# A four-layer graph-attention kernel: the setup in an order of its own

## The chip, the core and the metric

The kernel runs on one core of one Trainium2 chip. The metric is the device time of one execution in microseconds, as a median over several runs. The kernel before takes 2730.86 us (median of 3 runs, 2729.93 to 2731.75). A profile of one execution shows a span of 2728.8 us.

The core has five engines [...]: TensorE (PE, matrix products and transposes; its weight loads are counted apart as PEld), VectorE (DVE), ScalarE (ACT), GpSimd (POOL) and SyncE (SP). SyncE issues most transfers here; ScalarE can issue them too. [...]

## What is computed

`x` is 16 graphs of 1024 nodes with 256 features, `adj` is one 1024 x 1024 matrix of int32, shared by all graphs. Four layers follow each other; each normalises x, applies a ReLU, runs a graph attention and adds the result to x. Layer 0 looks like this; the others differ in heads (4, 1, 4, 1), in the slope, in the test on `adj` and in the last function:

```python
h = jnp.maximum(_layernorm(x, axis=-1), 0.0)
q = (h @ W).reshape(B, N, H, D)
e_src = jnp.einsum('bnhd,d->bnh', q, a_src)
e_dst = jnp.einsum('bnhd,d->bnh', q, a_dst)
e = e_src[:, :, None, :] + e_dst[:, None, :, :]
e = jnp.where(e >= 0, e, ALPHA * e)
e = jnp.where(mask, e, NEG_INF)        # adj > 0 in layers 0, 1; adj != 0 in layers 2, 3
attn = jax.nn.softmax(e, axis=2)
h_prime = jnp.einsum('bijh,bjhd->bihd', attn, q)
x = x + jax.nn.elu(h_prime)            # relu in layer 3
```

## The kernel before

**Steps and streams.** One step is one layer of one graph, 64 steps in all. Four graphs are in work at a time ("streams"); `order_of_steps` interleaves them, so the order begins with layer 0 of streams 0, 1, 2, then layer 1 of stream 0, layer 0 of stream 3, layer 1 of stream 2, layer 2 of stream 0.

**A step** has three parts. Its *preparation* (L159) has 20 pieces: statistics of x on VectorE and ten small operations on GpSimd (`stats`, L166), normalising on ScalarE (`xn`, L193), transposes on TensorE with the ReLU on ScalarE (`hT`, L201, L202), the products with the weights (`project`, L213, evacuated by ScalarE into `whx` and `sd`), then exponentials of the attention logits (`factors`) and a small transpose whose result goes to DRAM (`grow`) and comes back as a row broadcast to all partitions (`gs`, L258; copied into PSUM as `g`, L264). Its *aggregation*: VectorE makes tiles of attention weights `w` (L269, 128 x 1024, eight to a head) out of `g`, the column factors and a mask; TensorE multiplies them with `whx` (L285). Its *finish* (L306 to L328) divides, applies the last function and adds to x.

**Order by hand.** All this is emitted under a manual schedule. Index 8n + k is the group k of step n, eight to each step. An agenda gives each piece of a preparation its index (`agenda_of`), normally one to two steps ahead; `emit_tiles` sends tiles of w ahead as far as 18 buffers (`WBUFS`) allow; `finish` of a step lies in the first groups of the next. The two first preparations have index -99, so both are emitted whole before the first group.

**The setup** stands ahead of this loop and is not part of the manual schedule. First, for each of the four layers: load the weights W, load the two attention vectors broadcast to all partitions (`a_bc`, on ScalarE's queue), make extra columns of W out of them on VectorE (four products, L104, and four sums, L106), and get a bound on the logits: a square (`sq`, L111), two products with a matrix of ones (`pn`, L114), a maximum, a root on GpSimd and three small products, which give `cbias`, `nbias`, `rbias`. Then the masks, in eight row blocks of `adj`: load 128 rows, clamp to -1, 0, 1 as `sgn` (L134), eight transposes into PSUM (L137), and two compares on VectorE (L139), greater than zero for layers 0 and 1 and not equal to zero for layers 2 and 3. Last, the loads of x for the four streams. The two setup parts have pools of their own, released before the pools of the main part are made, so that memory of the first is used again by the second.

Of the kernel before, what the change touches and what calls it, by code (L numbers as in the profile page):

```python
# [23 lines left out]
F32 = mybir.dt.float32  # L24
BF16 = mybir.dt.bfloat16
I32 = mybir.dt.int32
U8 = mybir.dt.uint8
AF = mybir.ActivationFunctionType
ALU = mybir.AluOpType
AX = mybir.AxisListType  # L30
PSUM = bass.MemoryType.PSUM

P = 128
EPS = 1e-5
SHIFT = 60.0
STREAMS = 4
WBUFS = 18
# [11 lines left out]
LAYERS = [  # L49
    (4, 0.2, 0, 0),  # L50
    (1, 0.2, 0, 0),
    (4, 0.2, 128, 1),
    (1, 0.01, 0, 1),
]
# [3 lines left out]
def kernel(ctx: ExitStack, tc: tile.TileContext, x, adj, ws, avs, out):  # L58
    nc = tc.nc
    B, N, F = x.shape  # L60
    C = N // P
    K = F // P
    HALF = C // 2

    const = ctx.enter_context(tc.tile_pool(name="const", bufs=1))

    ident = const.tile([P, P], F32, name="ident")
# [3 lines left out]
    half1 = const.tile([P, 1], F32, name="half1")  # L71
    nc.gpsimd.memset(half1, 0.5)
    ones = const.tile([P, P], F32, name="ones")
    nc.gpsimd.memset(ones, 1.0)

    masks = [const.tile([P, C, N], U8, name=f"mask{i}") for i in range(2)]
    wx = []
# [3 lines left out]
    nbias = [const.tile([P, 1], F32, name=f"nbias{l}") for l in range(len(LAYERS))]  # L81
    rbias = [const.tile([P, 1], F32, name=f"rbias{l}") for l in range(len(LAYERS))]
    cbias = [const.tile([P, 1], F32, name=f"cbias{l}") for l in range(len(LAYERS))]
    shift60 = const.tile([P, 1], F32, name="shift60")
    nc.gpsimd.memset(shift60, SHIFT)


    with tc.tile_pool(name="wprep", bufs=2) as wp, tc.tile_pool(
        name="wpsum", bufs=2, space=PSUM
    ) as wps:  # L90
        for l, (H, slope, hs, _) in enumerate(LAYERS):
            D = F // H
            nc.sync.dma_start(out=wx[l][:, :, 0:F], in_=ws[l].rearrange("(k p) f -> p k f", p=P))
            a_bc = wp.tile([P, 2, H, D], F32, name="a_bc")
            for part in range(2):
                nc.scalar.dma_start(
                    out=a_bc[:, part],
                    in_=bass.AP(tensor=avs[l].tensor, offset=avs[l].offset + part * D,
                                ap=[[0, P], [hs, H], [1, D]]),
                )  # L100
            for k in range(K):
                for part in range(2):
                    prod = wp.tile([P, H, D], F32, name="prod")
                    nc.vector.tensor_mul(  # L104
                        prod, wx[l][:, k, 0:F].rearrange("p (h d) -> p h d", h=H), a_bc[:, part])
                    nc.vector.tensor_reduce(  # L106
                        wx[l][:, k, F + part * H:F + (part + 1) * H], prod, AX.X, ALU.add)

            sq = wp.tile([P, K, H], F32, name="sq")
            wd = wx[l][:, :, F + H:F + 2 * H]  # L110
            nc.vector.tensor_tensor(sq, wd, wd, op=ALU.mult)  # L111
            pn = wps.tile([P, H], F32, name="pn")
            for k in range(K):
                nc.tensor.matmul(pn, lhsT=ones, rhs=sq[:, k, :], start=(k == 0),  # L114
                                 stop=(k == K - 1))
            bound = wp.tile([P, 1], F32, name="bound")
            nc.vector.tensor_reduce(bound, pn, AX.X, ALU.max)
            nc.gpsimd.tensor_tensor(bound, bound, half1, op=ALU.pow)
            nc.vector.tensor_scalar(cbias[l], bound, 16.01, None, op0=ALU.mult)
            nc.vector.tensor_scalar(nbias[l], bound, -16.01 * slope, None, op0=ALU.mult)  # L120
            nc.vector.tensor_scalar(rbias[l], bound, -16.01 * (1.0 - slope), SHIFT,
                                    op0=ALU.mult, op1=ALU.add)


    with tc.tile_pool(name="mprep", bufs=2) as mp, tc.tile_pool(
        name="mpsum", bufs=2, space=PSUM
    ) as mps:
        identb = mp.tile([P, P], BF16, name="identb", bufs=1)
        nc.vector.tensor_copy(identb, ident)
        for ic in range(C):  # L130
            a_raw = mp.tile([P, N], I32, name="a_raw")
            nc.sync.dma_start(out=a_raw, in_=adj[ic * P:(ic + 1) * P, :])
            sgn = mp.tile([P, N], BF16, name="sgn")
            nc.vector.tensor_scalar(sgn, a_raw, -1.0, 1.0, op0=ALU.max, op1=ALU.min)  # L134
            pm = mps.tile([P, C, P], BF16, name="pm")
            for jc in range(C):
                nc.tensor.transpose(pm[:, jc, :], sgn[:, jc * P:(jc + 1) * P], identb)  # L137
            for m, op in ((0, ALU.is_gt), (1, ALU.not_equal)):
                nc.vector.tensor_scalar(masks[m][:, :, ic * P:(ic + 1) * P], pm, 0.0, None, op0=op)  # L139

    xpool = ctx.enter_context(tc.tile_pool(name="xpool", bufs=STREAMS))
    prep = ctx.enter_context(tc.tile_pool(name="prep", bufs=2))
    small = ctx.enter_context(tc.tile_pool(name="small", bufs=4))
    work = ctx.enter_context(tc.tile_pool(name="work", bufs=2))
# [5 lines left out]
    L = len(LAYERS)  # L150
    steps = order_of_steps(B, L)
    xs = {}
    state = [dict() for _ in steps]

    def load(b):
        xs[b] = xpool.tile([P, C, F], F32, name="x")
        nc.sync.dma_start(out=xs[b], in_=x[b].rearrange("(c p) f -> p c f", p=P))
# [198 lines left out]
    def prepare(upto):  # L356

        while agenda and agenda[0][0] <= upto:
            _, n, piece, last = agenda.pop(0)
            piece()  # L360
            if last:
                done["prepared"] = n + 1

    def plan(n):
        new = preparation(n)
        agenda.extend((at, n, piece, i == len(new) - 1) for i, (at, piece) in enumerate(new))
        agenda.sort(key=lambda a: a[:2])
# [11 lines left out]
    def emit_tiles(upto, must=False):  # L379
        while done["tiles"] < min(upto, len(tiles)):  # L380
            i = done["tiles"]

            while done["g"] <= min(i + C // 2, len(tiles) - 1):
                n, h, _ = tiles[done["g"]]
                if n >= done["prepared"]:
                    if i < done["g"] or not must:
                        break
                    prepare(max(a[0] for a in agenda if a[1] == n))
                broadcast(n, h)
                done["g"] += C  # L390
                fetch_heads()
            if i >= done["g"]:
                return
            weights(*tiles[i])
            done["tiles"] += 1

    for b in range(STREAMS):
        load(b)
    last, agenda_of = {}, []
    for n, (b, l) in enumerate(steps):  # L400

        free = 8 * (last[b % STREAMS] + 1) + (8 if l == 0 else 5) if b % STREAMS in last else -99
        last[b % STREAMS] = n
        start = 8 * (n - 2)
        before = [LAYERS[steps[max(n - i, 0)][1]][0] for i in (0, 1, 2)]
        if before[2] == 1:
            kind = SOON if before[:2] == [4, 1] else AFTER_ONE
        else:
            kind = SOON if l == 0 else AFTER_FOUR
        if free > start + kind[0]:  # L410
            kind = LATE
            start = max(free, agenda_of[-1][0] + 5)
        agenda_of.append([start + k if n > 1 else -99 for k in kind])
        if n > 2:

            was = agenda_of[n - 1]
            assert agenda_of[n][2] >= was[4] and agenda_of[n][3] >= was[10]
    ending = []
    with tc.manual_schedule():
        for planned in (1, 2):  # L420
            plan(planned - 1)
            prepare(-1)
        for n in range(len(steps)):
            for k, (h, i0, per) in enumerate(groups(n)):
                while planned < len(steps) and agenda_of[planned][0] <= 8 * n + k:
                    plan(planned)
                    planned += 1
                emit_tiles(place[n, h, C - 1] + 1, must=True)
                aggregate(n, h, i0, per)
                if i0 + per == C:  # L430
                    done["free"] = place[n, h, C - 1] + 1
                while ending and ending[0][0] <= k:
                    ending.pop(0)[1]()
                prepare(8 * n + k)
                ahead = 6 if per > 1 else 3
                emit_tiles(min(done["tiles"] + ahead, done["free"] + WBUFS))
            for _, piece in ending:
                piece()
            ending = finish(n)
        for _, piece in ending:  # L440
            piece()
# [33 lines left out]
```

## Time and profile before

| what | value |
|---|---|
| median, lowest, highest of 3 runs | 2730.86, 2729.93, 2731.75 us |
| span of the profiled execution, mean clock of TensorE | 2728.8 us, 0.987 |
| TensorE busy | 2569.4 us (94%) |
| TensorE weight loads | 2269.7 us (83%) |
| VectorE busy | 1909.6 us (70%) |
| ScalarE busy | 1220.6 us (45%) |
| GpSimd busy | 985.5 us (36%) |
| largest group: products L285 | 1950.3 us, 36864 of them, 242 ns each |
| largest on VectorE: tiles w, L269 | 1544.6 us, 1280 of them, 1277 ns each |
| x of the four streams, issue | from 58.24 us, 4 of 1024 KB |

A busy share is an average over stages with different limits. Where it matters which engine sets the pace, one reads stretches of the time axis, and for each stretch the engine that has no idle time, or the wait that ends last.

### The profile page before, as it was taken

Reading aid. Unit: us, or ns where it says so; the run is one execution under the profiler, and the core shown is the slowest. Engines: PE = TensorE matmul, PEld = TensorE weight load, DVE = VectorE, ACT = ScalarE, POOL = GpSimd, SP = SyncE. Lnnn points to the kernel's source line nnn. Section 1 sums busy time; section 2 is a strip of 40 time slices with the busy share of each in tenths; the row PEclk is TensorE's granted clock in tenths of the full one; section 3 lists DMA queues with packets and bytes.
Section 4 is the critical chain, followed back from the end, with each engine's and each line's share of the span. In section 5 each row is a group of like instructions: output and inputs, shape, how many; then the busy total and the mean of one; then the engine's idle time right before and its main releaser. Section 6 shows DMA issues by size and latency. Waiting matters only on the chain.

```text
span 2728.8 us, 89586 instructions
## 1 busy us (share of the span) xinstructions
PE 2569.4 (94%) x40080; PEld 2269.7 (83%) x40080; DVE 1909.6 (70%) x2061; ACT 1220.6 (45%) x3329; POOL 985.5 (36%) x1230
## 2 busy tenths in 40 slices
PE   1699999999999999999999999999999999999998
PEld 1488888888888888888888888888888888788876
DVE  5396866667874878757877668747787567678752
ACT  0434445444454454454444544544435444444431
POOL 0224334334234344353242353433332443443321
PEclk9899999999999999999999999999999999999999
DMA  4110010011211111002211211002112110011111
GB/s 133 61 58 23 28 41 33 18 56 49 73 56 40 56 64 35 24 32 71 73 33 48 63 41 42 33 17 72 59 46 72 50 47 25 33 41 42 33 33 54
DMA packets 63679, 130.13 MB, mean 48 GB/s; under 512 B 6208, under 2 KB 41792, under 8 KB 63296
## 3 DMA queue, kind: packets, MB, share of 16 engines
q1 hardware_dynamic: 60608, 123.35, 13.6%
q8 instruction: 316, 5.18, 0.8%
q10 hardware_dynamic: 2688, 1.05, 0.1%
q14 instruction: 67, 0.55, 0.1%
HBM read 106.95 MB, written 17.43 MB: 46 GB/s over the span
## 4 chain that ended last, share of the span: by engine, by line
PE 81%; DVE 8%; ACT 4%; issue 4%; POOL 2%; DMA 1%; DVEq 0%; ACTq 0%; SPq 0%; POOLq 0%
PE acc L285 61%; PE pp L213 16%; DVE w L269 6%; PE pp L201 4%; ACT xn L193 1%; DVE bn L171 1%; POOL rstd L184 1%; DMA a_bc<-in_L_gnn_a 1%; ACT whx L215 1%; ACT e L319 0%; ACT g L264 0%; DVE mask L139 0%; ACT whx L219 0%; PE pp L240 0%; ACT whx L222 0%
## 5 line engine op out<-in xcount | busy, mean ns | idle before, releaser
L285 PE MATMUL acc<-whx,w 128*64 128x65 f32 x36864 | 1950.3, 242 | 42.2 <-DVE w L269 31.7
L285 PEld LDWEIGHTS acc<-whx,w 128*64 128x64 f32 x36864 | 1766.0, 145 | 225.4 <-issue 73.7
L269 DVE SCALAR_TENSOR_TENSOR w<-g,rcol,mask 128x1024 f32<-128x1024 f32 x1280 | 1544.6, 1277 | 482.8 <-ACT g L264 435.7
L289 ACT ACTIVATE y<-acc 128x260 f32<-128x260 f32 (+1 forms) x512 | 196.5, 384 | 1090.4 <-PE acc L285 1090.4
L213 PE MATMUL pp<-wx,hT 128*128 128x258 f32 (+1 forms) x2048 | 513.0, 394 | 5.6 <-ACT hT L202 4.4
L310 POOL TENSOR_TENSOR y<-y,r 128x1024 f32<-128x1024 f32 x128 | 242.3, 1897 | 614.2 <-DVE r L306 614.2
L213 PEld LDWEIGHTS pp<-wx,hT 128*128 128x128 f32 x2048 | 374.7, 191 | 76.4 <-ACT hT L202 7.3
L326 POOL TENSOR_TENSOR x<-x,e 128x1024 f32<-128x1024 f32 x96 | 226.7, 2366 | 278.0 <-DVE e L325 258.4
L224 POOL TENSOR_TENSOR whx<-whx 128x256 f32<-128x256 f32 x256 | 159.8, 629 | 457.0 <-ACT whx L222 456.1
L193 ACT ACTIVATE xn<-x,shift,rstd 128x256 f32<-128x256 f32 x512 | 264.0, 590 | 122.7 <-POOL shift L187 122.5
L325 DVE SCALAR_TENSOR_TENSOR e<-e,y 128x1024 f32<-128x1024 f32 x96 | 118.2, 1232 | 196.9 <-ACT e L319 196.9
L215 ACT ACTIVATE whx<-pp,nbias 128x4 f32<-128x4 f32 (+1 forms) x512 | 135.0, 264 | 165.3 <-PE pp L213 153.9
L201 PE MATMUL pp<-ident,xn 128*128 128x128 f32 x1024 | 158.3, 286 | 51.1 <-ACT xn L193 41.3
L201 PEld LDWEIGHTS pp<-ident,xn 128*128 128x128 f32 x1024 | 116.1, 143 | 91.2 <-ACT xn L193 52.0
L171 DVE BATCH_NORM_STATS2 bn<-x 128x6 f32<-128x256 f32 x512 | 173.2, 411 | 5.6 <-DMA x<-in_x 2.8
L264 ACT ACTIVATE g<-gs 128x1024 f32<-128x1024 f32 x160 | 162.3, 1018 | 5.2 <-DVE w L269 5.1
L202 ACT ACTIVATE hT<-pp 128x512 f32<-128x512 f32 x256 | 142.9, 592 | 16.1 <-PE pp L201 13.8
L178 POOL TENSOR_TENSOR dev<-bn 128x8 f32<-128x8 f32 x64 | 16.3, 255 | 308.4 <-DVE bn L171 308.4
L219 ACT ACTIVATE whx<-pp,whx 128x256 f32<-128x256 f32 x256 | 121.5, 474 | 0.0
L319 ACT ACTIVATE e<-e 128x1024 f32<-128x1024 f32 x96 | 100.8, 1050 | 30.1 <-POOL e L315 30.1
L184 POOL TENSOR_TENSOR rstd<-rstd,neghalf 128x8 f32<-128x8 f32 x64 | 106.6, 1666 | 5.0
L315 POOL TENSOR_SCALAR e<-y 128x1024 f32<-128x1024 f32 x96 | 99.9, 1040 | 8.5
(44 smaller groups left out, 552.7 us busy)
## 6 DMA issues: line engine op xcount, KB each, us to landing
gs<-grow SPq DMA_DIRECT2D x160, 512.0 KB
x<-in_x SPq DMA_DIRECT2D x16, 1024.0 KB
out<-x SPq DMA_DIRECT2D x32, 512.0 KB
a_raw<-in_adj SPq DMA_DIRECT2D x8, 512.0 KB
a_bc<-in_L_gnn_a ACTq DMA_DIRECT2D x8, 128.0 KB
wx<-in_L_gnn_W SPq DMA_DIRECT2D x4, 256.0 KB
grow<-gT SPq DMA_DIRECT2D x32, 16.0 KB
grow<-gT SPq DMA_DIRECT2D x32, 4.0 KB
```

Source lines behind the costliest of these rows:

```text
L171: nc.vector.bn_stats(bn[:, c, :], xs[b][:, c, :])
L193: nc.scalar.activation(xn[:, q, :], xs[b][:, c, :], AF.Identity, bias=st["shift"][:, c:c + 1], scale=st["rstd"][:, c:c + 1])
L201: nc.tensor.transpose(pt[:, q, :], st["xn", half][:, q, k * P:(k + 1) * P], ident)
L213: nc.tensor.matmul(pw, lhsT=st["hT", half][:, k, q * P:(q + 1) * P], rhs=wx[l][:, k, :], start=(k == 0), stop=(k == K - 1))
L215: nc.scalar.activation(whx[:, c, :, D], pw[:, F + H:F + 2 * H], AF.Exp, bias=nbias[l], scale=slope)
L224: nc.gpsimd.tensor_tensor(whx[:, c, :, 0:D], whx[:, c, :, 0:D], whx[:, c, :, D:D + 1].to_broadcast([P, H, D]), op=ALU.mult)
L264: nc.scalar.activation(g, state[n]["gs", h], AF.Copy)
L269: nc.vector.scalar_tensor_tensor(w, state[n]["g", h], state[n]["rcol"][:, jc, h:h + 1], masks[LAYERS[steps[n][1]][3]][:, jc, :], op0=ALU.m ...
L285: nc.tensor.matmul(acc[o % P:o % P + cols, q, :], lhsT=st["w", h, jc][:, o:o + cols], rhs=st["whx"][:, jc, h, :], start=(jc == 0), stop=(j ...
L289: nc.scalar.activation(st["y"][:, i0:i0 + per, h, :], acc, AF.Copy)
L310: nc.gpsimd.tensor_tensor(yh, yh, r[:, :, None].to_broadcast([P, HALF * H, D]), op=ALU.mult)
L326: nc.gpsimd.tensor_add(xh, xh, e)
```

## The change

The setup is taken apart and emitted under the manual schedule as well, in an order of its own. Five things change:

1. x of stream 0 is the first transfer; then come W and the vectors of layer 0 and x of stream 1. The streams 2 and 3 are loaded after step 1's preparation, together with the weights of the other layers.
2. `adj` is loaded in column blocks (128 columns of all rows, in rows of 512 bytes) on ScalarE's queue. A block goes straight into one row of the mask.
3. Only the first mask is made by a compare on VectorE. The second, not equal to zero, is the square of the same values (-1, 0, 1), made by ScalarE out of the same PSUM tile.
4. The mask blocks are interleaved with the preparation of step 0: three blocks before its first transposes, three between its parts, two after it. Step 1's preparation follows in halves, with the eight first tiles of w between them.
5. The extra columns and bounds of layers 1, 2 and 3 are made in the loop: vectors, columns and bound of layer 1 at index 1, 2, 3; of layer 2 at 29, 30, 31 (the last groups of step 3); of layer 3 at 45, 46, 47 (the last groups of step 5). Their small constants go to GpSimd.

The separate pools are gone: blocks of `adj` and `sgn` use buffers of `w`, the transposed block a PSUM buffer of `acc`, the vectors a buffer of `e`, the bound one of `pp`. The purpose is that the engines work side by side in the setup, and that what the first step doesn't need comes later.

```diff
-    with tc.tile_pool(name="wprep", bufs=2) as wp, tc.tile_pool(
...
-    with tc.tile_pool(name="mprep", bufs=2) as mp, tc.tile_pool(
...
-            for m, op in ((0, ALU.is_gt), (1, ALU.not_equal)):
-                nc.vector.tensor_scalar(masks[m][:, :, ic * P:(ic + 1) * P], pm, 0.0, None, op0=op)
+    def weight_columns(l):
...
+        def vectors():
+            st["a"] = prep.tile([P, HALF, H, D], F32, name="e")
+            for part in range(2):
+                nc.sync.dma_start(
...
+        def columns():
...
+        def bound():
+
+            pn = ps_p.tile([P, H], F32, name="pp")
...
+        def fetch_block():
+            st["raw"] = work.tile([P, C, P], I32, name="w", bufs=WBUFS)
+            nc.scalar.dma_start(out=st["raw"], in_=adj.rearrange("(c p) j -> p c j", p=P)[
+                :, :, jc * P:(jc + 1) * P])
...
+        def mask():
+            pm = st["pm"].rearrange("p c i -> p (c i)")
+            nc.vector.tensor_scalar(masks[0][:, jc, :], pm, 0.0, None, op0=ALU.is_gt)
+            nc.scalar.activation(masks[1][:, jc, :], pm, AF.Square)
...
-    for b in range(STREAMS):
-        load(b)
...
-        agenda_of.append([start + k if n > 1 else -99 for k in kind])
+        agenda_of.append([start + k for k in kind] if n > 1 else [-2] * 10 + [-1] * 10)
...
+        load(0)
+        load_weights(0)
+        layer[0][0]()
+        for jc in range(C):
+            blocks[jc][0]()
+        load(1)
+        nc.vector.tensor_copy(identb, ident)
+        first = [piece for _, piece in preparation(0)]
+        first[0]()
+        first[1]()
+        layer[0][1]()
+        layer[0][2]()
+        first[2]()
+        first[3]()
+        for jc in range(3):
+            for piece in blocks[jc][1:]:
+                piece()
+
+        for i, jc in ((4, 3), (6, 4), (10, 5), (12, None), (14, None)):
...
+        for piece in first[16:]:
+            piece()
+        for jc in range(6, C):
+            for piece in blocks[jc][1:]:
+                piece()
+        done["prepared"] = 1
+        plan(1)
+        planned = 2
+        prepare(-2)
+        emit_tiles(C, must=True)
+        prepare(-1)
+        for i in range(1, STREAMS):
+            load_weights(i)
+            if i > 1:
+                load(i)
+
+        for l, at in ((1, 1), (2, 8 * 3 + 5), (3, 8 * 5 + 5)):
+            for i, piece in enumerate(layer[l]):
+                later[at + i] = piece
...
+                if 8 * n + k in later:
+                    later[8 * n + k]()
                 prepare(8 * n + k)
```

## The prediction

> **What bounds the kernel now.** I read the page's slices first, to see where TensorE is not full; then a table of busy times by stretch over the first 300 us; then VectorE in order of time; then the waits of the setup.
>
> ```profile
> PE   1699999999999999999999999999999999999998
> DVE  5396866667874878757877668747787567678752
> ...
> 0.00:32.00 32.00, 4.03 (x16) 3.71 (x16) 12.60 (x49) 0.00 (x0) 2.67 (x14) 1.00 0.23 66
> 32.00:58.00 26.00, 7.50 (x64) 6.42 (x64) 19.95 (x25) 0.00 (x0) 0.51 (x1) 1.00 0.47 161
> 58.00:72.00 14.00, 0.21 (x2) 0.00 (x0) 9.43 (x20) 1.61 (x2) 3.54 (x10) 1.00 0.92 292
> 72.00:90.00 18.00, 13.85 (x49) 9.30 (x49) 0.00 (x0) 11.59 (x40) 5.79 (x13) 1.00 0.02 7
> 90.00:110.00 20.00, 13.34 (x49) 9.04 (x49) 0.00 (x0) 11.65 (x39) 7.50 (x14) 0.74 0.18 54
> 110.00:121.00 11.00, 3.50 (x29) 2.27 (x28) 9.65 (x9) 2.12 (x3) 0.00 (x0) 0.53 0.32 97
> 121.00:205.00 84.00, 75.84 (x2076) 70.60 (x2077) 84.00 (x84) 29.93 (x71) 22.59 (x34) 0.97 0.15 54
> 205.00:300.00 95.00, 91.43 (x1396) 79.73 (x1395) 70.53 (x73) 44.62 (x121) 38.90 (x44) 0.96 0.10 30
> ```
>
> A slice is 68 us. TensorE is full from the third slice to the last but one; only the first two have much room. In the table the columns are the stretch, its length, busy us (count) of PE, PE weight load, DVE, ACT, POOL, then clock, DMA share, GB/s. To 58 us ScalarE does nothing; from 72 to 110 VectorE does nothing: the setup is a relay. From 121 to 205 VectorE is busy 84.00 of 84 us, so the first three steps (four heads each) end when VectorE has made their tiles; after 205 TensorE is the bound again. So an earlier setup is worth what it moves the first tile of w, less what is added to VectorE before 205, plus any later hole in TensorE.
>
> ```profile
> 15.79 0.76 DVE L104 TENSOR_TENSOR prod<-wx,a_bc 128x256 f32<-128x256 f32 x2 [5.79 <-DMA a_bc<-in_L_gnn_a]
> ...
> 38.35 4.62 DVE L139 TENSOR_SCALAR mask<-pm 128x1024 uint8<-128x1024 bf16 x4
> ...
> 64.66 2.71 DVE L171 BATCH_NORM_STATS2 bn<-x 128x6 f32<-128x256 f32 x8 [2.65 <-DMA x<-in_x]
> ...
> 111.35 9.63 DVE L269 SCALAR_TENSOR_TENSOR w<-g,rcol,mask 128x1024 f32<-128x1024 f32 x8 [41.07 <-ACT g L264]
> 120.89 2.70 DVE L171 BATCH_NORM_STATS2 bn<-x 128x6 f32<-128x256 f32 x8
> ```
>
> Columns of all layers wait for vectors until 15.79; sixteen mask writes take 1.16 us each (4.62/4); the first x is read at 64.66; the first tile of w starts at **111.35**, after an idle of 41.07.
>
> [...]
> - [...] the copy g takes 1.00 to 1.02 us. I use 1.05 for Square. Both programs hold one table load.
> - [...] The column blocks of adj have rows of just 512 B; the kernel before has rows of 4 KB (adj) and 1 KB (x, at about 350 GB/s), so nothing here shows 512 B.
> - [...] The trace has both queues in the first 16 us, at a mean of 84 GB/s (1.34 MB), with the second vector of layer 0 landing 14.5 us after its issue.
>
> **The change, part by part** (T is the time of the first sgn; I write the rest as T + us).
>
> *When T is.* x is issued first and beside it W0, two vectors, half of adj. About 2 MB must move before x is in; at 300 GB/s after a start of 2 us (x: issued 58.24, flowing at 60) that is about 9 us, so stats end at 12, the ten POOL operations (4.2 us, 67.45 to 71.64) at 17, xn (4.04) at 21. Not binding. The second vector landed at 15.79; it now queues behind x and W0, so I take 17 (12 to 26). From its landing to the reduced bound the trace took 4.1 us with another layer's work between; I take 3.6. **T = 20.6.**
>
> *Masks.* A block is sgn 0.69, eight transposes 1.05, compare 1.16, in VectorE's order one after the other: 2.95 us. Compares end at 2.95, 5.9, 8.8; Square of the third at 9.9. The second compare of each block (8 x 1.16) is gone from VectorE, but waits for transposes take its place, so this alone gains little. The gain is in what now lies beside it.
>
> *Step 0's preparation, interleaved.* hT after the third Square: 11.0. Block 3's Square 12.75. Four projections at ScalarE's cadence of 0.89 (84.76, 85.65, 86.61, 87.50): 15.9. Block 4: 18.35. hT: 19.4. Block 5: 21.3. Four more projections: 24.5; factors 0.9, row transposes and gT: 26.0. Blocks 6 and 7 follow on TensorE, so the last compare ends at 30.9. The gs transfer starts at about 28 and hides behind all that follows.
>
> *Step 1's first half.* Its stats are queued behind the last compare: 33.6; POOL 37.9; from the first xn to the fourth projection the trace took 10.5 to 10.95 us: 48.9; the broadcast g 1.0: tiles start at T + 50 = **70.6**, against 111.35. Gain **40.8**. Step 1's second half (ends T + 57) lies beside tiles that end at T + 59.5, so costs nothing.
>
> *x of stream 2* is now issued only after step 1's rows. On SyncE: rows T + 57.1 (0.7 issue), W1 and W2 (0.45 each), x2 at about 59.3. In the trace the first x landed 6.4 us after its issue among four; I take 5.5, so 64.8. VectorE's next instruction after the eight tiles (T + 59.5) is step 2's stats on that x, and behind it stand head 1's tiles: VectorE stands **5.3** us (0 to 10).
>
> *Layer 1's columns* sit in VectorE's row after the 20th tile: eight operations of 0.42 and two of 0.16, **3.7** us, in the stretch where VectorE has no idle. Their vectors are issued some 15 us earlier. The TensorE product and POOL operations are in its shadow.
>
> *Layer 2's columns* come near the end of step 3, where VectorE has slack (it waits 6.45 us for a buffer at 305), but their product stands in TensorE's queue right after step 3's last matmul, ahead of step 5's transposes. By the trace (times of before) VectorE would reach them at 287.5 and end at 291.0; TensorE is idle from 286.6 to 288.95 already and resumes aggregation at 291.12. Product and transposes then give 292.7: **1.6**; up to 6 if the vectors (issued about 278) land as slowly as the first ones.
>
> *Layer 3's columns* fall after the third tile of step 6, made at 368.4 to 378.0; TensorE already waits for these tiles at 378.18 and VectorE is full from 376 to 420 (44.00 of 44). So all 3.6 us count: **3.6**.
>
> Everything after that stands in the same order on each engine in both programs, so its time is unchanged. Constants moved from VectorE to POOL (four small operations) are hidden behind the masks.
>
> Sum: 40.8 - 5.3 - 3.7 - 1.6 - 3.6 = 26.6. 2730.9 - 26.6 = **2704.3**.
>
> **The rivals.**
> - *Setup starved by transfers.* For: 512-byte rows, two queues at once, and the measured 130 GB/s between 8 and 12 us. Then 3.5 MB needs some 27 us; the vectors land near 29 and T is 33: 12.4 us less gain, **2717**. Against: x alone reached 350 GB/s with 1 KB rows.
> - *Nothing is given back.* x2 lands in time because its 1 MB flows at 350 GB/s in 3 us with little else, and the columns of layers 2 and 3 fit into TensorE's existing holes: 40.8 - 3.7 - 1 = 36, **2695**. Against: VectorE's full stretch from 376 to 420.
> - *Slower than before.* If all loads run at the 84 GB/s of the first 16 us, the vectors are in at 42, tiles at about 96 (gain 15); x2 behind 1.5 MB takes 18 us more (stall 18); columns cost 8.9, and late vectors stall each of three insertions by another 5 us: 15 - 18 - 9 - 15 = -27, **2758**. Against: those 16 us held 256-byte pieces of one address, and in the same trace layer 2's vector was used 4.5 us after its issue.
>
> **How the numbers follow.** Likeliest 0.62, starved 0.18, nothing given back 0.15, slower 0.05. The range takes in the middle of both neighbouring cases, with T from 15 to 34, the stall from 0 to 10 and the late columns from 1 to 10 not all at one end: 2691 to 2719. It leaves out the slower case and about a third of the two neighbours. A change of 0.2% is 5.5 us: faster 0.93, same 0.02, slower 0.05.
>
> **What would show it.** First tile of w near 71 us; one wait of VectorE's stats for x of 3 to 8 us right after eight tiles; a wait of TensorE's product for sq at the end of step 3; VectorE full to about 175 instead of 205; the same span from there on. It is wrong if the vectors of layer 0 land after 26 us, if a block of adj is waited for between compares, or if TensorE shows a hole over 5 us behind one of the three products.

## The result and the profile after

On one chip the changed kernel takes 2716.61 us (2713.68 to 2718.09, 4 runs) against 2730.39 us (2729.61 to 2731.75, 4 runs) for the kernel before: a ratio of **0.9948**, 95% interval 0.993 to 0.9965, 13.8 us less. The forecast was 26.6 us less. The profiled execution has a span of 2711.9 us against 2728.8, so 16.9 us less. The direction was right, the time lies near the slow end of the stated range (2691 to 2719), and half of the gain is missing.

The page's slices of the kernel after, 68 us each:

```profile
PE   3799999999999999999999999999999999999998
DVE  3796686477875688666876778748687567678752
```

TensorE's first two digits are 3 and 7 where the kernel before had 1 and 6; from the third slice on its digits are the same. The table of stretches (length, busy us of PE, PE weight load, DVE, ACT, POOL, then clock, DMA share, GB/s) says how:

```profile
32.00:58.00 26.00, 16.06 (x97) 12.26 (x97) 10.14 (x12) 17.31 (x45) 4.87 (x8) 1.00 0.07 21
58.00:78.00 20.00, 10.37 (x32) 7.05 (x32) 3.26 (x9) 9.16 (x24) 6.01 (x14) 0.57 0.14 48
...
112.00:175.00 63.00, 59.64 (x1601) 55.71 (x1599) 62.83 (x65) 23.20 (x57) 16.75 (x18) 0.96 0.18 61
175.00:205.00 30.00, 27.55 (x610) 23.86 (x608) 30.00 (x36) 18.45 (x48) 12.94 (x24) 1.00 0.02 5
```

The relay is gone: between 32 and 58 us ScalarE is busy for 17.31 us, where before it did nothing. VectorE is still full up to 205, where the prediction had 175. But 205 was only the edge of a row in the prediction's table: in the kernel before VectorE goes on, with gaps of 0.22 us at most, until it waits for a `g` at 239.3 us. In the kernel after the same wait begins at 217.2, 22 us earlier. The two waits, before and after:

```profile
248.56 9.63 DVE L269 SCALAR_TENSOR_TENSOR w<-g,rcol,mask 128x1024 f32<-128x1024 f32 x8 [9.26 <-ACT g L264]
224.60 9.62 DVE L289 SCALAR_TENSOR_TENSOR w<-g,rcol,mask 128x1024 f32<-128x1024 f32 x8 [7.42 <-ACT g L284]
```

VectorE of the kernel after in order of time (start, length, then the idle time before it and what ended it):

```profile
7.76 2.71 DVE L191 BATCH_NORM_STATS2 bn<-x 128x6 f32<-128x256 f32 x8 [6.03 <-DMA x<-in_x]
...
21.93 0.43 DVE L124 TENSOR_TENSOR e<-wx,e 128x256 f32<-128x256 f32 x1 [7.05 <-DMA e<-in_L_gnn_a]
...
78.25 9.62 DVE L289 SCALAR_TENSOR_TENSOR w<-g,rcol,mask 128x1024 f32<-128x1024 f32 x8 [16.98 <-ACT g L284]
96.01 2.71 DVE L191 BATCH_NORM_STATS2 bn<-x 128x6 f32<-128x256 f32 x8 [8.14 <-DMA x<-in_x]
```

x of stream 0 is there at 7.8 us, earlier than I had assumed (stats were to end at 12). The second vector of layer 0, though, lands at 21.93 instead of 17, the first `sgn` starts at T = 25.84 instead of 20.6, the first tile of `w` at **78.25** instead of 70.6, and the wait for x of stream 2 is 8.14 us instead of 5.3.

The waits of the first 130 us (engine and line, what was waited for, us in total, times, the longest) name one more that was in no step of mine:

```profile
ACT L213 <- DMA w<-in_adj: 29.6, 1, 29.6
...
DVE w L289 <- ACT g L284: 17.0, 1, 17.0
```

ScalarE in order of time shows what it is:

```profile
0.72 28.82 ACTq L155 DMA_DIRECT2D w<-in_adj  x8
29.56 1.28 ACT L213 ACT_TABLE_LOAD   x1 [29.56 <-DMA w<-in_adj]
30.86 4.04 ACT L213 ACTIVATE xn<-x,shift,rstd 128x256 f32<-128x256 f32 x8
```

ScalarE issues the eight blocks of `adj` first. One issue takes between 0.48 and 9.63 us, the whole row 28.82, and why some take that long is not shown. Its first computation starts at 29.56 us, although `shift` for `xn` was ready at 14.8. Behind `xn` stand the Squares, and the third block's transposes wait 5.29 us for a Square.

**Where the lead is won and lost.** From step 6 on both programs have the same order on every engine, so I take one instruction there, the statistics that start at 443.54 us in the kernel before and at 425.90 in the kernel after. There the changed kernel is 17.6 us ahead. Its way there: first tile 33.1 ahead (111.35 - 78.25); head 1's tiles 24.9 (123.50 - 98.64); after layer 1's columns 21.5; ahead of layer 2's columns 24.0 (248.56 - 224.60); behind them 21.1; after layer 3's columns 17.6. So 33.1 - 8.2 - 3.4 + 2.5 - 2.9 - 3.5 = 17.6. The 2.5 us won on the way stand in no step of the prediction; where they come from is told with the columns, further below. This lead at 443.5 us is the measure for the experiments, since the work behind it is common to all of them.

### The profile page after: what moved, and what is told of

It is laid out like the page before. It is cut to its first block, busy times and chain, and to the rows that moved or that the text cites. A ratio compares the mean times of both kernels' runs of the same rounds, so it can differ in the third digit from the quotient of the medians.

```text
span 2711.9 us, 89498 instructions
## 1 busy us (share of the span) xinstructions
PE 2567.2 (95%) x40080; PEld 2269.2 (84%) x40080; DVE 1900.3 (70%) x2041; ACT 1229.6 (45%) x3337; POOL 992.3 (37%) x1242
## 4 chain that ended last, share of the span: by engine, by line
PE 81%; DVE 8%; ACT 4%; issue 3%; POOL 2%; DMA 1%; ACTq 0%; DVEq 0%; SPq 0%; POOLq 0%
PE acc L305 61%; PE pp L233 16%; DVE w L289 6%; PE pp L221 4%; ACT xn L213 1%; DVE bn L191 1%; DMA w<-in_adj 1%; ACT whx L235 1%; ACT g L284 1%; POOL rstd L204 0%; ACT e L339 0%; POOL y L330 0%; ACT whx L239 0%; PE pp L260 0%; DMA x<-in_x 0%
## 5 line engine op out<-in xcount | busy, mean ns | idle before, releaser
L305 PE MATMUL acc<-whx,w 128*64 128x65 f32 x36864 | 1951.0, 242 | 42.0 <-DVE w L289 28.6
L305 PEld LDWEIGHTS acc<-whx,w 128*64 128x64 f32 x36864 | 1766.8, 145 | 225.2 <-issue 70.4
L244 POOL TENSOR_TENSOR whx<-whx 128x256 f32<-128x256 f32 x256 | 159.9, 630 | 444.9 <-ACT whx L242 443.5
L191 DVE BATCH_NORM_STATS2 bn<-x 128x6 f32<-128x256 f32 x512 | 172.9, 407 | 16.9 <-DMA x<-in_x 14.2
L222 ACT ACTIVATE hT<-pp 128x512 f32<-128x512 f32 x256 | 143.2, 592 | 18.5 <-PE pp L221 16.5
L339 ACT ACTIVATE e<-e 128x1024 f32<-128x1024 f32 x96 | 100.8, 1050 | 33.1 <-POOL e L335 33.1
```

Of the source, the lines that this page charges most:

```text
L191: nc.vector.bn_stats(bn[:, c, :], xs[b][:, c, :])
L244: nc.gpsimd.tensor_tensor(whx[:, c, :, 0:D], whx[:, c, :, 0:D], whx[:, c, :, D:D + 1].to_broadcast([P, H, D]), op=ALU.mult)
L305: nc.tensor.matmul(acc[o % P:o % P + cols, q, :], lhsT=st["w", h, jc][:, o:o + cols], rhs=st["whx"][:, jc, h, :], start=(jc == 0), stop=(j ...
```

## The experiments

Two theories explain the missing part. **A**: it sits in the waits just named, and each can be taken away by itself. **B**: it was lost to TensorE's granted clock, which is 0.57 between 58 and 78 us, where step 1's first half is prepared; the kernel before has 1.00 and 0.64 in the two stretches with the same work (71.67 to 82.40 and 92.97 to 103.30). **C**, a rival for single steps: transfers collide, or the chain of masks and products binds anyway, so that removing a wait only uncovers the next.

All results in one table. "First tile" and "wait" are from each profile, "lead" is the lead over the kernel before at 443.5 us, "gain" is the median against the kernel before on the same chip (2734.87 us for e1 to e4, 2732.99 for e0 and e5 to e7, 2731.70 for e8 and e9).

| kernel | first tile | wait for x of stream 2 | lead | median | gain | ratio, 95% interval |
|---|---|---|---|---|---|---|
| changed | 78.25 | 8.14 | 17.6 | 2716.61 | 13.8 | 0.9948 (0.993 to 0.9965) |
| e0 changed again | 77.90 | 7.70 | 17.2 | 2716.06 | 16.9 | 0.9933 (0.9921 to 0.9945) |
| e1 x early | 78.08 | none | 23.7 | 2707.06 | 27.8 | 0.9902 (0.9888 to 0.9915) |
| e2 adj split | 73.69 | 7.23 | 24.6 | 2710.75 | 24.1 | 0.9915 (0.9901 to 0.9928) |
| e3 one vector | 67.60 | 8.23 | 28.2 | 2704.82 | 30.1 | 0.9892 (0.9878 to 0.9905) |
| e4 columns in the gap | 77.27 | 4.78 | 27.9 | 2705.55 | 29.3 | 0.9896 (0.9882 to 0.991) |
| e5 all four | 64.57 | none | 44.1 | 2688.83 | 44.2 | 0.9831 (0.9818 to 0.9843) |
| e6 two compares | 80.39 | 7.59 | 15.1 | 2718.35 | 14.6 | 0.9947 (0.9935 to 0.9958) |
| e7 masks first | 83.59 | 7.79 | 12.0 | 2717.53 | 15.5 | 0.9944 (0.9931 to 0.9956) |
| e9 statistics early | 72.19 | 7.57 | 25.6 | 2705.92 | 25.8 | 0.9902 (0.9888 to 0.9916) |
| e8 all four and e9 | 60.27 | none | 50.1 | 2680.62 | 51.1 | 0.9809 (0.9795 to 0.9822) |

### e3: both vectors in one transfer

```diff
-            for part in range(2):
-                nc.sync.dma_start(
-                    out=st["a"][:, part],
-                    in_=bass.AP(tensor=avs[l].tensor, offset=avs[l].offset + part * D,
-                                ap=[[0, P], [hs, H], [1, D]]),
-                )
+            size = 2 * F if H == 1 or hs else 2 * D
...
+            nc.sync.dma_start(out=st["a"][:, 0:size],
+                              in_=bass.AP(tensor=avs[l].tensor, offset=avs[l].offset,
+                                          ap=[[0, P], [1, size]]))
```

For layer 0 this is one transfer of 128 pieces of 512 bytes in place of two with 512 pieces of 256 bytes each; the four heads read the one copy. The vectors of the other layers become one transfer each as well, of 2 KB pieces.

> The two attention vectors of a layer come in one transfer of 128 pieces of 512 B (layer 0) or 2 KB instead of 2 x 512 pieces of 256 B (layers 0 and 2) or 2 x 128 of 1 KB. Theory A1 (the small pieces of one address are slow, and hold up what shares the engines): the vector lands about 8 us earlier, T falls from 25.8 to 15 to 18, the dip to 50 to 130 GB/s between 10 and 18 us goes; ScalarE's transfer issues also end earlier, by about 20 us; first tile of w 5 to 8 us earlier, 2709 to 2712. Theory A2 (the vectors are late because they queue behind x and W0 and beside adj, whatever their size): T stays above 23 and the time within 2 us of the changed kernel.

Measured: the first `sgn` at 15.01 us, 10.8 earlier, the first tile 10.65 earlier, the lead 28.2 instead of 17.2 to 17.6. VectorE's line no longer shows a wait for the vectors. The stretches 10 to 12 and 14 to 16 us, last number GB/s, first in the kernel after:

```profile
10.00:12.00 2.00, 0.00 (x0) 0.00 (x0) 0.47 (x2) 0.00 (x0) 1.05 (x5) 1.00 0.21 51
14.00:16.00 2.00, 0.00 (x0) 0.00 (x0) 0.84 (x2) 0.00 (x0) 0.66 (x3) 1.00 0.46 131
```

and then in e3:

```profile
10.00:12.00 2.00, 0.00 (x0) 0.00 (x0) 1.93 (x7) 0.00 (x0) 1.17 (x5) 1.00 1.13 337
14.00:16.00 2.00, 1.14 (x7) 1.06 (x8) 0.76 (x2) 0.00 (x0) 1.83 (x5) 1.00 1.16 291
```

The packets of the traces tell what the wait was made of. x and W of layer 0 are issued ahead of the vectors on the same queue; they move at up to 346 GB/s, and x is in at 7.8 us in both kernels. In the kernel after no piece of a vector moves before 7.60 us, where before the first one moves at 2.60. The 1024 pieces then start one after the other until 21.48, for 13.9 us (before: 2.60 to 15.38, 12.8 us). In e3 the 128 pieces begin as late, at 7.84, but the last one starts at 9.43. So the queue ahead of the vectors costs 5.0 us, and stays; what e3 takes away is the slow passage of the pieces, during which `adj`, issued by another engine, crawls as well (51 and 131 GB/s in all, in the two stretches above).

Neither their size nor their number is enough to explain it, since layer 2's vectors are 1024 pieces of 256 bytes too. The packets of the kernel before from 4 to 7.5 us (layer 0's vectors, with next to nothing beside them) and from 18.5 to 21.2 us (layer 2's), then those of the kernel after from 2.5 to 7.5 us; some packets of 4 bytes are counted under 512 B:

```profile
DMA packets 278, 0.07 MB, mean 21 GB/s; under 512 B 273, under 2 KB 278, under 8 KB 278
DMA packets 1056, 0.26 MB, mean 97 GB/s; under 512 B 1056, under 2 KB 1056, under 8 KB 1056
DMA packets 1992, 1.58 MB, mean 315 GB/s; under 512 B 16, under 2 KB 1992, under 8 KB 1992
```

Layer 2's pieces pass in 2.5 us (18.62 to 21.10, and 256.20 to 258.75 in the kernel after). In the program they differ in where they are read: each transfer of layer 2 reads four addresses 128 times, each of layer 0 reads one address 512 times. That makes 80 and 74 pieces per us for layer 0, before and after, and 80 for the one address of e3, with pieces twice as large, but about 400 for layer 2. My estimate from these figures is that one address gives some 80 pieces per us, of 256 as of 512 bytes. No run changes the addresses alone, so this cause is likely but not shown.

### e2: half of adj issued by SyncE

```diff
-            nc.scalar.dma_start(out=st["raw"], in_=adj.rearrange("(c p) j -> p c j", p=P)[
+            queue = nc.scalar if jc < C // 2 else nc.sync
+            queue.dma_start(out=st["raw"], in_=adj.rearrange("(c p) j -> p c j", p=P)[
```

> Blocks 4 to 7 of adj are issued by SyncE instead of ScalarE. Theory A: ScalarE is no longer held in its own transfer issues until 29.6 us; its table load and xn run at about 15 to 20 us, the first Square no longer waits behind xn, the wait of 5.3 us of the third block's transposes for Square goes; T stays at 25.8, the first tile of w comes about 2.5 us earlier (75.8), 2714. Theory C (the masks' chain through VectorE, TensorE and ScalarE binds anyway): first tile within 1 us of 78.25 and no change.

Measured, ScalarE in order of time:

```profile
11.92 1.28 ACT L214 ACT_TABLE_LOAD   x1 [11.92 <-issue]
14.82 4.04 ACT L214 ACTIVATE xn<-x,shift,rstd 128x256 f32<-128x256 f32 x8 [1.61 <-POOL shift L208]
28.00 1.02 ACT L172 ACTIVATE mask<-acc 128x1024 uint8<-128x1024 bf16 x1 [9.15 <-DVE mask L171]
```

`xn` now waits only for GpSimd, and the first Square waits for VectorE's compare instead of the other way round. The first `sgn` comes at 24.93, 0.9 us earlier, and from there to the first tile it takes 48.8 us instead of 52.4. The first tile is 4.6 us earlier, so ScalarE's hold cost 3.6 us of the chain from T. The lead is 7.0 greater; 5.5 of it are there at head 1's tiles (93.17 against 98.64). The rest appears at layer 2's columns, where the granted clock is 0.93 in e2 and 0.87 in the profile of the changed kernel, so it isn't a gain of the edit.

### e1: x of streams 2 and 3 and the later weights loaded earlier

```diff
         for piece in first[16:]:
             piece()
+        for i in range(1, STREAMS):
+            load_weights(i)
+            if i > 1:
+                load(i)
...
         prepare(-1)
-        for i in range(1, STREAMS):
-            load_weights(i)
-            if i > 1:
-                load(i)
```

> x of streams 2 and 3 and the weights of layers 1 to 3 are issued after step 0's rows instead of after step 1's. Theory A (the missing gain sits in named waits): VectorE's wait of 8.14 us for x at the statistics of step 2 is gone, first tile of w stays at 78 us, so 8 us faster than the changed kernel: about 2708.5. Theory B (the gain is lost to TensorE's granted clock, 0.50 to 0.73 between 58 and 112 us, so that what VectorE gains TensorE gives back): under 3 us, 2714 or more, with the mean clock unchanged at 0.981 to 0.984. Theory C (transfers collide): the gs row lands later, the first tile moves beyond 80 us and half of the 8 us is lost again.

Measured: the first tile doesn't move, and step 2's statistics follow the eight tiles without any wait:

```profile
78.08 9.62 DVE L289 SCALAR_TENSOR_TENSOR w<-g,rcol,mask 128x1024 f32<-128x1024 f32 x8 [16.88 <-ACT g L284]
87.63 2.70 DVE L191 BATCH_NORM_STATS2 bn<-x 128x6 f32<-128x256 f32 x8
```

Head 1's tiles start at 90.25 instead of 97.85 (e0) or 98.64, and the lead is 6.0 to 6.4 us greater. Of the 7.6 to 8.4 us at head 1 some 1.4 go back into a new wait of VectorE for a `w` buffer at 135.66 us, `[1.41 <-PE acc L305]`: there TensorE has become the slower one. A wait uncovered by taking away another is what C says in its second half, but it is 1.4 us of 8 only; of colliding transfers, the first half of C, there is no sign, since the first tile stays at 78.08.

### e4: the columns of layers 1 to 3 in VectorE's gap

```diff
-        agenda_of.append([start + k for k in kind] if n > 1 else [-2] * 10 + [-1] * 10)
+        agenda_of.append([start + k for k in kind] if n > 1 else [-3] * 2 + [-2] * 8 + [-1] * 10)
...
+        for i in range(1, L):
+            load_weights(i)
+            layer[i][0]()
...
+        prepare(-3)
+        for l in range(1, L):
+            layer[l][1]()
...
-        for l, at in ((1, 1), (2, 8 * 3 + 5), (3, 8 * 5 + 5)):
-            for i, piece in enumerate(layer[l]):
-                later[at + i] = piece
+        for l in range(1, L):
+            later[l] = layer[l][2]
```

The vectors are issued behind step 0's rows, the columns stand behind step 1's statistics; only the bounds stay in the loop, at index 1, 2 and 3.

> The columns of layers 1, 2 and 3 are made in VectorE's idle 17 us between step 1's statistics and the first tile of w (their weights and vectors issued after step 0's rows); their bounds at index 1, 2, 3. x of streams 2 and 3 stays late. Theory A: the 3.4 us of layer 1 and 3.5 us of layer 3 are saved, and TensorE's wait of 4.4 us at the end of step 3; against these, the first tile may come up to 2 us later if a vector is late: 5 to 7 us faster than the changed kernel, about 2710.5. Theory B (clock): under 3 us.

Measured: the columns run from 62.52 to 72.4, wholly inside the idle time that ends at 77.27:

```profile
77.27 9.62 DVE L290 SCALAR_TENSOR_TENSOR w<-g,rcol,mask 128x1024 f32<-128x1024 f32 x8 [4.28 <-ACT g L285]
91.68 2.71 DVE L192 BATCH_NORM_STATS2 bn<-x 128x6 f32<-128x256 f32 x8 [4.78 <-DMA x<-in_x]
```

The lead is 10.2 to 10.6 us greater. Part comes from the wait for x, which is 2.9 to 3.4 us shorter; the likely reason is that W1 and W2 no longer stand ahead of x on SyncE's queue. Another 1.6 us go with a granted clock of 1.00 at layer 2's old place. Most of the rest comes from the columns. The stretch of layer 3 shows it purest: between 324 and 409 us (times of before) e4 keeps its lead of 27.9, while the changed kernel falls from 21.1 to 17.7.

### e5: the four together, and e0, the control

> The changed kernel once more, unaltered, as the control for the others on this chip. If the ratio of 0.9948 to the kernel before is a property of the program, it comes again within its interval (0.993 to 0.9965), with the first tile of w at 78.2 us and a stall of 8.1 us for x of stream 2. Theory B (the missing part was lost to the clock of TensorE) expects the ratio to move with the granted clock: a mean clock of 0.984 or more gives 0.994 or less, one of 0.981 gives 0.996.

> All four repairs at once: both vectors in one transfer, half of adj issued by SyncE, x of streams 2 and 3 loaded right behind the vectors, the columns of layers 1 to 3 in VectorE's gap ahead of the first tile. Theory A (the missing gain sits in the named waits, and they add up): reduced bound at 15.0 as with one vector, first tile 48.8 us later as with the split adj, so at 63.8 us, 14.5 earlier than in the changed kernel; no stall for x (8.1) and no columns among tiles (3.4 + 0.3 + 3.5): 29.7 us faster than the changed kernel. Theory C (transfers collide, and the chain of masks and step 1 binds anyway): the early loads delay blocks of adj and with them compares; first tile at 68 us or later, and the whole no more than 20 us faster than the changed kernel.

e0 gives 0.9933, inside the expected interval. Its lead at 443.5 is 17.2, as good as the changed kernel's 17.6, but its profiled span is 2717.0 and not 2711.9: the two executions of one program drift apart by 5 us behind 443.5, where nothing was changed, with mean clocks of 0.983 and 0.984.

e5, VectorE in order of time:

```profile
64.57 9.63 DVE L295 SCALAR_TENSOR_TENSOR w<-g,rcol,mask 128x1024 f32<-128x1024 f32 x8 [4.44 <-ACT g L290]
74.11 2.70 DVE L197 BATCH_NORM_STATS2 bn<-x 128x6 f32<-128x256 f32 x8
```

The first tile comes at 64.57, against 63.8 expected by A and 68 or later by C; the time is 27.2 us below e0 (2716.06 - 2688.83), against 29.7 and at most 20. The lead is 26.9 greater. So the waits add up, nearly: 2.5 us are missing to 29.7, and the 0.8 at the first tile and two new waits of VectorE for TensorE, 1.79 us at 92.97 and 1.75 at 121.16, are more than enough for them. And with 0.54 between 40 and 58 us the granted clock is low here too, so the first tile's gain doesn't come from it.

### e6: the second mask by a compare again

```diff
-            nc.scalar.activation(masks[1][:, jc, :], pm, AF.Square)
+            nc.vector.tensor_scalar(masks[1][:, jc, :], pm, 0.0, None, op0=ALU.not_equal)
```

> Undoes one part: the second mask is a second compare on VectorE again, no Square on ScalarE. The prediction said that the shared masks alone gain little. VectorE has 8 x 1.16 = 9.3 us more; in the first three blocks it runs while ScalarE is still held in its own transfers until 29.6 and normalises until 34.9, so these three cost nothing; the other five cost up to 1.16 each where VectorE binds. First tile 0 to 5.8 us later than in the changed kernel, 2 us taken. A rival: since the transposes of the third block now wait for no Square behind ScalarE's late start, the first tile comes up to 3 us earlier.

Measured: first tile at 80.39, 2.5 us later than in e0, lead 2.1 less, median 2.3 more; the intervals of e0 and e6 overlap, so the times alone don't tell them apart. Eight compares are 9.3 us more of VectorE's time, and a quarter of it reaches the first tile. Of the parts that were undone or moved here, the shared masks are worth least.

### e7: all masks ahead of step 0

```diff
-        for jc in range(3):
+        for jc in range(C):
             for piece in blocks[jc][1:]:
                 piece()
...
-        for piece in first[16:]:
+        for piece in first[4:]:
```

> Undoes one part: all eight mask blocks stand ahead of the transposes and products of step 0, nothing interleaved. The last compare then comes some 3 us earlier (54 us), but step 0's transposes, products and factors (12 us) stand behind it and ahead of step 1's statistics: first tile at about 87 us, 8.6 later than in the changed kernel, and the whole later by as much. If the interleaving is worth nothing, because VectorE has room beside it, the first tile comes within 2 us of 78.2.

Measured: the last compare starts at 51.72 instead of 57.27 and the first tile at 83.59, 5.7 us later than in e0 and not 8.6; the lead is 5.2 less. The chain was not the one I had written. Step 1's statistics follow the last compare at once, at 52.86, since nothing of step 0 stands ahead of them on VectorE; but their ten small operations on GpSimd stand behind step 0's products with `whx`, and `xn` starts at 71.79, 3.48 us after ScalarE is free. The medians (2717.53 against 2716.06, intervals overlapping) show less than the profiles do; the six runs of e7 spread from 2714.95 to 2723.78 and the profiled one is the slowest. How much the interleaving is worth in the time, between 1.5 and 5.7 us, stays open.

### e9 and e8: step 1's statistics ahead of the last two mask blocks

```diff
                 blocks[jc][2]()
                 blocks[jc][3]()
+            if i == 10:
+                plan(1)
+                for _ in range(2):
+                    agenda.pop(0)[2]()
...
-        plan(1)
```

> The changed kernel with one thing moved: step 1's statistics stand ahead of the last two mask blocks on VectorE instead of behind them. The prediction had put the first tile on the chain last compare, statistics, GpSimd, normalising, products. If that chain binds: VectorE has 5.3 us of waiting there, so the statistics cost the compares nothing; xn then starts when ScalarE has written the last Square (59.6) instead of at 65.6, and the first tile, the eight tiles and x of stream 2 (issued behind step 1's rows) all come 6.0 us earlier: TensorE 6.0 us further ahead at 444 us, the time some 6 us less. If it doesn't bind (a rival: ScalarE or the products of step 0 do), the first tile moves by less than 2 us.

> The kernel with the four repairs, with step 1's statistics moved in the same way. There xn could start at 45.9 instead of 52.1 and the first tile at 58.4 instead of 64.6; but the columns of layers 1 to 3 stand in VectorE's row ahead of the first tile and end at 60.1, since their vectors land at 49.6. So the first tile comes at 60.2, 4.4 us earlier, and the time is some 4 us less than with the four repairs: a ratio near 0.9815 to the kernel before. If the columns' vectors, now not hidden, come later or TensorE and not VectorE sets the pace behind, 0 to 2 us.

e9 is the changed kernel with this edit, e8 is e5 with it. The first tile, in e9:

```profile
72.19 9.62 DVE L289 SCALAR_TENSOR_TENSOR w<-g,rcol,mask 128x1024 f32<-128x1024 f32 x8 [13.63 <-ACT g L284]
```

and in e8:

```profile
60.19 0.16 DVE L136 TENSOR_TENSOR sq<-wx 128x2 f32<-128x2 f32 x1
60.27 9.62 DVE L295 SCALAR_TENSOR_TENSOR w<-g,rcol,mask 128x1024 f32<-128x1024 f32 x8
```

In e9 the first tile is 5.7 to 6.1 us earlier, as expected (6.0), and the last compare, at 57.33, is as early as in e0 (57.27): the statistics fit into VectorE's wait for TensorE. The lead is 8.0 to 8.4 us greater. Of that, 5.8 to 6.6 us are there at head 1's tiles. The rest, about 2 us, appears between 195 and 324 us and goes with the granted clock there, which differs from profile to profile (told with the columns below): the two profiles of the changed kernel alone have leads of 21.5, 23.9, 21.1 and 22.3, 22.2, 20.7 in that stretch. In e8 the first tile comes at 60.27 (60.2 expected), directly behind the last operation of the columns: `g` was ready earlier, and VectorE itself is now the bound. The lead is 6.0 greater than in e5, where 4.4 at the first tile and 4 in the time were expected: 4.3 are there at the first tile, and the waits of 1.79 and 1.75 us for TensorE have shrunk to one of 0.91. At **2680.62 us** e8 is the fastest kernel of this study, 36 us below the changed one.

## Why the prediction was right in direction and too high in size

The sum of the prediction, term by term, in us:

| step | forecast | measured | shown by |
|---|---|---|---|
| T, first `sgn` | 20.6 | 25.84 | e3: 15.01 with one transfer |
| first tile after T | 50 | 52.4 | e2: 48.8 without ScalarE's hold |
| gain at the first tile | 40.8 | 33.1 | |
| wait for x of stream 2 | 5.3 | 8.14 | e1: none |
| layer 1's columns | 3.7 | 3.4 | lead before and after |
| layer 2's columns | 1.6 | 2.9; 1.3 to 1.5 at a like clock | twelve profiles, below |
| granted clock between 186 and 221 us | none | 2.5 won; nothing in e0 | twelve profiles, below |
| layer 3's columns | 3.6 | 3.4 to 3.5 | e4 and e5 lose nothing there |
| sum | 26.6 | 17.6 | lead at 443.5 us |

**The step that was off most is the landing of the vectors**: 4.9 of the 9.0 us that are missing in the lead. The prediction had them queueing "behind x and W0" and took 17, 1.2 us more than the 15.79 of the kernel before. The queue was the right mechanism, mis-sized: the first piece moves 5.0 us later than before (7.60 against 2.60), and the passage takes 13.9 us instead of 12.8, so the second vector is used at 21.93. The prediction did know that these pieces are slow, since it discounted the 84 GB/s of the first 16 us before as "256-byte pieces of one address". But it used that only to argue against its slowest rival, and didn't add their whole passage behind x and W0.

The size of the pieces alone doesn't explain this: `adj` in rows of 512 bytes flows at 291 GB/s in e3 (14 to 16 us). Layer 2's vectors in pieces of 256 bytes move at about 100, while layer 0's pieces, of the same 256 bytes, move at 21 GB/s with next to nothing beside them (both in the kernel before); that factor of five is not one of size. So the rival "setup starved by transfers" met the time (2717) by luck: it had T at 33 instead of 25.84, and it blamed the 512-byte rows.

**"Not binding" was wrong for `xn`.** The data were ready at 14.8, better than the 17 assumed, but ScalarE wasn't: it stood in its own transfers until 29.56. The prediction followed the data of `xn` and left out what stands ahead of it in ScalarE's row. With eight transfers of 512 KB there, halving that row in e2 brings the first tile 4.6 us forward. The cost of this step in the chain from T was 3.6 us; without it the first tile comes 48.8 us after T, against the 50 forecast.

**The wait for x** was the right wait at the right place, and mis-sized by 2.8 us. It was issued at 87.45 and read at 96.01, 8.6 us later, where I had taken 5.5 and the trace of before had 6.4. The weights W1 to W3 are issued around it, at 86.46 and 87.96, and x of stream 3 at 88.58. In e4, without the weights there, the wait is 2.9 to 3.4 us shorter; which of these neighbours slowed it is not separated.

**The columns** were right in all three layers, and none of the signs that the prediction had named for being wrong appears: the vectors landed before 26 us, VectorE waits for no block of `adj`, and TensorE's longest hole at one of the three products is 4.44 us. For layer 2, TensorE does wait for `sq` at the end of step 3, as forecast:

```profile
267.12 1.02 PE L137 MATMUL pp<-sq,ones 128*128 128x4 f32 x4 [4.44 <-DVE sq L131]
```

Its price has to be read at a like clock. The stretch between the same two evacuations of `acc` around these columns, in the kernel before, in e0 and in the kernel after (the third number from the end is the granted clock):

```profile
283.19:306.03 22.84, 19.82 (x305) 16.55 (x304) 16.09 (x17) 11.12 (x28) 9.38 (x14) 0.93 0.01 2
261.04:285.30 24.26, 19.72 (x309) 16.50 (x308) 19.19 (x27) 11.12 (x29) 11.12 (x18) 0.93 0.01 2
259.24:284.90 25.66, 21.00 (x309) 18.15 (x308) 19.35 (x27) 11.24 (x29) 11.12 (x18) 0.87 0.01 2
```

At 0.93 the columns cost 1.4 us. All twelve profiles fit: without columns in the stretch it takes 22.8 to 22.9 us at 0.93 (before, e5, e8), with them 24.1 to 24.3 at 0.93 (e0, e1, e2, e3, e7, e9) and 25.3 to 25.7 at 0.87 (the changed kernel, e6); e4, without them and at 1.00, takes 21.2. So the columns cost 1.3 to 1.5 us, and the lower clock cost the changed kernel 1.4 more in its profile.

The 2.5 us won ahead of it go with the clock too. The stretch of five evacuations there, before and after:

```profile
185.98:220.77 34.79, 29.89 (x673) 26.25 (x668) 34.57 (x42) 12.94 (x32) 11.04 (x20) 0.90 0.05 20
164.45:196.81 32.36, 28.08 (x673) 25.04 (x668) 32.36 (x40) 12.94 (x32) 9.05 (x15) 0.95 0.07 21
```

Six profiles have 0.90 here and take 34.4 to 35.0 us (before, e0, e1, e4, e7, e8), the other six have 0.95 and take 32.4 to 33.9. Both clocks occur for one and the same program, the changed kernel and e0, so this gain was luck of one execution.

**What the times add.** All eleven gains in the table agree with the lead at 443.5 us to within 4.2 us; the changed kernel and e1 are the two ends (13.8 for 17.6, and 27.8 for 23.7). Behind that point the executions drift by some us either way, with the same number of instructions on every engine. The means of whole runs are too coarse to say why: the changed kernel has clocks of 0.984, 0.982, 0.981 and 0.981 for 2713.68, 2718.09, 2717.86 and 2715.37 us. The twelve profiles say more. From that point to the end, the four with the highest mean clock there (0.992 to 0.993: e1, e9, before, after) take 2281.5 to 2286.0 us, and the eight others (0.989 to 0.991) 2287.3 to 2291.3. Two ends of it, e9 and e0:

```profile
417.93:2699.40 2281.47, 2218.02 (x34111) 1963.37 (x34109) 1608.40 (x1699) 1052.02 (x2869) 846.18 (x1027) 0.99 0.14 47
426.30:2717.00 2290.70, 2226.55 (x34111) 1970.03 (x34109) 1608.38 (x1699) 1051.97 (x2869) 845.88 (x1027) 0.99 0.15 47
```

TensorE needs 8.5 us more for the same 34111 products and transposes in e0, with VectorE's and ScalarE's times unchanged. So theory B is right for the drift between executions, some us in 2700, and not for the missing gain. The intervals of the changed kernel and e0 overlap, so their 13.8 and 16.9 us need no other cause.

## What to carry to other kernels

When a setup is rearranged, write for each engine its whole row of instructions, transfer issues included, and not only the chain of data: here ScalarE was held for 28.8 us by eight issues, and its first computation, whose data were ready at 14.8 us, came at 29.56. Cost a transfer by its pieces and by what stands ahead of it on its queue (5.0 us for the vectors here), with the rate that the same pieces had in the old trace, and look at how many of them read one address (80 pieces per us from one and 400 from four here, a likely cause, not a shown one); then ask what it does to the others in flight. Read the price of a small step from stretches with the same work and a like granted clock: layer 2's columns cost 1.3 to 1.5 us, and a clock of 0.87 instead of 0.93 added 1.4 in the same stretch. What comes later to clear the start has to be paid somewhere: put it where the engine has a wait ahead of the first bound, not into the stretch where that engine sets the pace.

## What was not expected of the hardware

- One broadcast slowed what was in flight with it: layer 0's vectors, 1024 pieces of 256 bytes and 256 KB in all, take 12.8 us before and 13.9 after, where the whole DMA traffic is 51 GB/s from 10 to 12 us and 131 from 14 to 16; with 128 pieces of 512 bytes in their place (e3) it is 337 and 291. Layer 2's vectors, as many pieces of the same size but from four addresses a transfer instead of one, pass in 2.5 us.
- A row of eight transfer issues held ScalarE for 28.8 us (0.72 to 29.56). In e3, where the same eight blocks flow faster, its first computation waits until 19.7 us, and in e2, with four of the issues, until 11.92.
- TensorE's granted clock is low while step 1's first half is prepared: 0.54 to 0.64 in before, after, e3, e5, e7, e8 and e9 alike. It is 0.57 from 65.6 to 77.2 us after, where the 28 transposes and products ahead of `g` take 9.71 us of PE time; in e7, at 0.62, the same 28 take 8.82, and `g` comes 0.9 us sooner after `xn`. But in the kernel before the same 28 take 8.90 at 1.00 and 8.51 at 0.64, so the mean clock alone doesn't tell the time of such short work. By my estimate from these figures, the size of theory B within the setup is about 1 us.
